# A four-layer network on one Trainium2 core: the last layer's preparation moved into the loop over layer 2's experts

## The chip, the cores and the metric

The kernel is one program on one core of a Trainium2 chip. The metric is device microseconds of one execution, the median of three runs. All data are float32. The core's engines each run their own queue of instructions: TensorE (PE, with its weight loads as PEld), VectorE (DVE), ScalarE (ACT), GpSimd (POOL) and SyncE (SP), which here only issues DMAs.

## The reference

A tensor of 16 sequences of 256 tokens with 128 features (4096 tokens) passes four layers. Each has the form `x = x + s * silu(f)`, where `s` is an attention-like branch and `f` a feed-forward branch, both computed from the same normalised `xn`. What matters here is the end of layer 2 and the whole of layer 3:

```python
# layer 2, feed-forward: mixture of 32 experts, the 4 best of a token weighted by their gate
gate = (one_hot(idx, E) * scores[..., None]).sum(-2)
h = relu(einsum('bsd,edh->bseh', x2, keys))
moe_out = einsum('bseh,ehd,bse->bsd', h, values, gate)
x = x + s * silu(src + moe_out)
# layer 3
xn = layernorm(x)
# branch s: two Mamba directions over layernorm(xn)
u = silu(conv(xn2 @ in_w)); dt = softplus(dbc[:64] @ dt_w + dt_b)
h_t = exp(dt * A) * h_{t-1} + dt * u * B_t     # 256 channels x 16 states
y = sum_n(h_t * C_t) + u * D;  s = xn + out_f + out_b
# branch f: 16 experts of 640 places, top 2 of a token, first come first served
probs = softmax(xn @ router_w + router_b);  vals, idx = top_k(probs, 2)
pos = cumsum(one_hot(idx)) - 1;  within = pos < 640
expert_inputs[idx, pos] = xn;  f = xn + shared(xn) + sum(vals * within * expert(...))
x = x + s * silu(f)
```

## The kernel before

The kernel is one class, `Net`. Four buffers of 16 KB per partition stay for the whole run: `x`, `xn`, `xnT` (features on partitions) and `s`. Tokens lie in 32 tiles of 128 (`NT`), or 8 chunks of 512 (`NCH`). Where nothing else is said, a planner orders the instructions of each engine: it goes by their order in the program, by what its own model of times says is ready, and by the buffers of the pools. Inside `manual_schedule` the named engines keep the order in which the program writes them.

**Experts of layer 2** (`ffn2`, from L1021). After attention, `norm_T` and a loop over chunks make the gates (L1045 to L1056). Then, for each chunk and each of 32 experts: one matmul to `f2_ph` (L1060), a ReLU on ACT to `f2_h` (L1064), four matmuls to `f2_po` (L1067) and four DVE sums into `acc`, weighted by the gate (L1072). `f2_ph` and `f2_po` have two buffers each, `f2_h` three. At the end of a chunk, `gate` (L111 to L113) applies SiLU and updates `x`. The planner orders all of this.

**Layer 3's first steps.** `norm_all` normalises `x` to `xn` and transposes it to `xnT` for all 32 tiles (L86 to L105). `route3` fills the DRAM buffers `xd` and `yd` with zeros and `md` with defaults (L1636, L1639, L1650), computes logits (L1669), softmax, the two best (L1682 to L1689), counts tokens per expert by two matmuls over all tiles at once (L1697, L1699) and one scan (L1707), and makes `at`, the destination row of each token and choice, and `meta`. `put_rows` (L1753) is one indirect DMA of 128 rows, issued by POOL: 64 carry rows of `xn` to `xd`, 64 rows of `meta` to `md`.

**Mamba** (`mamba3`, from L1308). It loads the weights of both directions (L69, L76), normalises `xn` a second time into `s` (L92), forms exp(A) (L1326), `taps` (L1331) and diagonals of D (L1336), issues 40 scatters, and enters a hand-written order for PE, DVE, ACT and POOL. `arrive` transposes a pair of sequences, `first` prepares one direction of a pair: it yields after each step so that a caller can place the steps. For the first direction both are run through in one go. Then the loop goes over 16 directions x 16 units; a unit has two scans (L1488, DVE), their factors two or three ahead (L1477, ACT), one product (L1462, POOL, two states ahead), one multiplication by C (L1599, DVE) and two sums on PE (L1603). Two steps of the next direction's `first` are put into each unit (`ahead`), what is left of them is put out at state 12, and one scatter goes behind every second unit. L1518 (`m_yg`) closes a direction.

**Last experts** (`ffn3`, from L1767) read `xd` and `md` and write the output.

Of the kernel before, what the change touches and what calls it, by code (L numbers as in the profile page):

```python
# [1 line left out]

# [5 lines left out]
F32 = mybir.dt.float32  # L8
# [24 lines left out]
class Net:  # L33
# [3 lines left out]
    def run(self):  # L37
        nc, tc = self.nc, self.tc
        with ExitStack() as ctx:
# [15 lines left out]
            with ExitStack() as two:  # L55
                c = two.enter_context(tc.tile_pool(name="l2c", bufs=1))
                with tc.tile_pool(name="l2a", bufs=1) as one:
                    self.norm_all()
                    bias, wqkv = self.layer1(one)
                    self.attn2(one, bias, wqkv)  # L60
                self.layer2(c)
            self.norm_all()
            self.layer3()
# [685 lines left out]
    def layer2(self, c):  # L749
        names = ("wqk2", "wv2", "wpbd", "hmask", "trig", "pe", "wo2", "ln1g", "ln1b", "ln2g", "ln2b", "selw")  # L750
        w = {n: self.load(c, n) for n in names}
        with self.tc.tile_pool(name="l2f", bufs=1) as one:
            self.ffn2(one, w)
# [267 lines left out]
    def ffn2(self, c, w):  # L1021
# [9 lines left out]
        self.relattn2(w, acc)  # L1031
        for g in range(0, NT, 8):
            self.norm(acc[:, g : g + 8, :], self.xn[:, g : g + 8, :], 8)
        with ExitStack() as ctx:
            sb = ctx.enter_context(tc.tile_pool(name="l2m", bufs=3))
            ps = ctx.enter_context(tc.tile_pool(name="l2m_ps", bufs=2, space=PSUM))
# [3 lines left out]
            for t in range(NCH):  # L1040
# [15 lines left out]
                nc.vector.tensor_tensor(gt[:, :, 0:NE], gt[:, :, 0:NE], rep[:, :, 0:NE], ALU.subtract)  # L1056
            for t in range(NCH):
                for e in range(NE):
                    ph = ps.tile([P, 512], F32, name="f2_ph")
# [3 lines left out]
                    hT = sb.tile([P, 512], F32, name="f2_h")  # L1063
# [11 lines left out]
                self.gate(sb, acc[:, 4 * t : 4 * t + 4, :], 4 * t, 4)  # L1075

# [222 lines left out]
    def layer3(self):  # L1299
        with ExitStack() as ctx:  # L1300
            keep = ctx.enter_context(self.tc.tile_pool(name="l3k", bufs=1))
            dram = ctx.enter_context(self.tc.tile_pool(name="l3x", bufs=1, space=DRAM))
            xd, md, yd, at, meta = self.route3(keep, dram)
            sent = [], []
            self.mamba3(self.scatter3(xd, md, at, meta, sent))
            self.ffn3(xd, md, yd, sent)

    def mamba3(self, scatter):  # L1308

        nc, tc = self.nc, self.tc
        N, T = 16, 2 * S
        with ExitStack() as ctx:
            c = ctx.enter_context(tc.tile_pool(name="l3c", bufs=1))
            lng, lnb = self.load(c, "lng3"), self.load(c, "lnb3")
            names = ("inT", "cb", "xpT", "dtT", "dtb", "A", "D", "outT")
            w = [{n: self.load(c, d + n) for n in names} for d in "fb"]
            one = self.ones[:, 0:1]  # L1320
            for g in range(0, NT, 8):
                self.norm(self.xn[:, g : g + 8, :], self.s[:, g : g + 8, :], 8)
            with tc.tile_pool(name="l3w0", bufs=1) as w0:
                for i, d in enumerate("fb"):
                    v = w[i]
                    nc.scalar.activation(v["A"], v["A"], AF.Exp)  # L1326
                    nc.vector.tensor_scalar_mul(v["A"], v["A"], -1.0)
                    taps = self.load_bc(w0, d + "cwr")
                    v["taps"] = c.tile([P, 4, 256], F32, name=d + "taps")
                    for j in range(4):  # L1330
                        nc.gpsimd.tensor_tensor(  # L1331
                            v["taps"][:, j, :], v["inT"][:, 0:256], taps[:, j * 256 : (j + 1) * 256], ALU.mult
                        )
                    v["Dd"] = c.tile([P, 2, P], F32, name=d + "Dd")
                    for k in range(2):
                        nc.vector.tensor_scalar_mul(v["Dd"][:, k, :], self.ident, v["D"][:, k : k + 1])  # L1336
            xp = [c.tile([P, 2, S + 3], F32, name=f"m_x{i}") for i in range(2)]
            for t in xp:
                nc.vector.memset(t[:, :, 0:3], 0.0)
            sb = ctx.enter_context(tc.tile_pool(name="l3a", bufs=2))  # L1340
            tmp = ctx.enter_context(tc.tile_pool(name="l3t", bufs=1))
            big = ctx.enter_context(tc.tile_pool(name="l3h", bufs=7))
            dram = ctx.enter_context(tc.tile_pool(name="l3d", bufs=3, space=DRAM))
            pp = ctx.enter_context(tc.tile_pool(name="l3pp", bufs=1, space=PSUM))
            factors = [pp.tile([P, 2, S], F32, name=f"m_a{n}") for n in range(3)]
            for t in factors:
                nc.vector.memset(t, 0.0)
            turn = [0]

            def arrive(p):  # L1350

                pt = pp.tile([P, 2, S], F32, name="m_pp")
                for t in range(4):
                    nc.tensor.transpose(
                        pt[:, t // 2, (t % 2) * P : (t % 2 + 1) * P], self.s[:, 4 * p + t, :], self.ident
                    )
                yield
                yield
                nc.vector.tensor_scalar(xp[0][:, :, 3:], pt, lng, lnb, ALU.mult, ALU.add)
                nc.vector.tensor_scalar(xp[1][:, :, 3:][:, :, ::-1], pt, lng, lnb, ALU.mult, ALU.add)  # L1360
                yield

            def first(p, i, st):

                v = w[i]
                uz = sb.tile([P, 4, T], F32, name="m_uz")
                u, z = uz[:, 0:2, :], uz[:, 2:4, :]
                st["u"], st["z"] = u, z  # L1370

                def inner(k):
                    pt = pp.tile([P, 2, S], F32, name="m_pp")
                    if k < 2:
                        for j in range(4):
                            nc.tensor.matmul(  # L1376
                                pt,
                                lhsT=v["taps"][:, j, k * P : (k + 1) * P],
                                rhs=xp[i][:, :, j : j + S],
                                start=j == 0,  # L1380
                                stop=j == 3,
                            )
                    else:
                        nc.tensor.matmul(
                            pt, lhsT=v["inT"][:, k * P : (k + 1) * P], rhs=xp[i][:, :, 3:], start=True, stop=True
                        )
                    return pt.rearrange("p b t -> p (b t)")
# [80 lines left out]
            def factor():  # L1468

                at = next(coming, None)  # L1470
                if at is None:
                    return
# [473 lines left out]
```

## Time and profile before

| | us |
|---|---|
| median of 3 runs | 4153.59 (4142.04 to 4166.65) |
| profiled execution, time | 4154.18 |
| profiled execution, span | 4152.5 |
| PE busy | 3635.0 (88%) |
| DVE busy | 2975.1 (72%) |
| ACT busy | 2133.2 (51%) |
| POOL busy | 1902.6 (46%) |
| layer 2's experts, L1060 to L1072 | 2325.0 to 2811.0 |
| first scan L1488 | 2940.7 |
| last multiplication by C, L1599, starts | 3928.5 |

The profile gives every instruction's engine, line, tiles, start and length, and what an idle engine waited for (`<-`). "x16" at the end of a line means that so many records were merged; a float32 matmul leaves two records, a transposition one. PEclk is the granted clock of TensorE as a share of full speed.

### The profile page before, as it was taken

How to read it: one execution, taken by the hardware profiler on the slowest of the kernel's cores; microseconds unless marked ns; L12 is line 12 of the kernel's file. 1: busy time of each engine (PE TensorE's matmuls, PEld its weight loads, DVE VectorE, ACT ScalarE, POOL GpSimd, SP SyncE). 2: the span in 40 equal slices, each digit the busy share in tenths (PEclk: the TensorE clock that was granted, in tenths of full speed). 3: DMA queues.
4: the chain of work that ended last, by engine and by line, in shares of the span. 5: the costliest groups of instructions: out<-in, count | busy, mean ns of one | idle time of the engine just before them, and what ended most of it. 6: DMA issues, size and time to landing. Idle time of an engine off the chain costs nothing.

```text
span 4152.5 us, 61388 instructions
## 1 busy us (share of the span) xinstructions
PE 3635.0 (88%) x21615; PEld 2306.3 (56%) x21615; DVE 2975.1 (72%) x6324; ACT 2133.2 (51%) x4635; POOL 1902.6 (46%) x1896
## 2 busy tenths in 40 slices
PE   5689999875999999999999999993798898899895
PEld 4477777543566666777777666662233333333353
DVE  5477777475888887666666666665698998999844
ACT  3356666642777775444445333331565665665422
POOL 5974444000444443433333000003889889877534
PEclk8899999986999999999999999995899999999998
DMA  8365554410000001000000000003211211211133
GB/s 305 126 218 180 195 198 161 59 62 6 1 1 1 1 1 41 1 1 1 1 1 1 1 1 1 1 1 132 94 70 63 82 62 62 82 62 61 56 92 102
DMA packets 87367, 268.91 MB, mean 65 GB/s; under 512 B 18176, under 2 KB 34088, under 8 KB 81555
## 3 DMA queue, kind: packets, MB, share of 16 engines
q1 hardware_dynamic: 80403, 255.46, 18.1%
q0 software_dynamic: 6656, 9.52, 0.7%
q8 instruction: 172, 2.82, 0.3%
q14 instruction: 136, 1.11, 0.1%
HBM read 192.96 MB, written 71.97 MB: 64 GB/s over the span
## 4 chain that ended last, share of the span: by engine, by line
PE 50%; DVE 25%; ACT 11%; issue 7%; POOL 5%; DMA 1%; SPq 0%; DVEq 0%; ACTq 0%; POOLq 0%
PE f_po L1067 6%; PE f_ph L1060 5%; DVE m_h L1488 4%; PE m_y L1603 4%; PE a_pp L906 3%; DVE r_mx L1164 3%; PE m_pp L1376 3%; ACT r_e L1170 2%; PE a_s L851 2%; DVE m_h L1599 2%; PE a_pp L345 2%; DVE a_e L397 2%; POOL xn_sb L170 2%; ACT m_a L1477 2%; PE r_pp L1194 2%
## 5 line engine op out<-in xcount | busy, mean ns | idle before, releaser
L1488 DVE TENSOR_TENSOR_SCAN m_h<-m_a,m_h 128x512 f32<-128x512 f32 x512 | 600.8, 1207 | 51.3 <-ACT m_a L1477 31.0
L1462 POOL TENSOR_TENSOR m_h<-m_B,m_dtu 128x1024 f32<-128x1024 f32 x256 | 597.4, 2358 | 63.6 <-PE m_y L1603 57.6
L1603 PE MATMUL m_y<-m_h,ident 128*128 128x512 f32 x1024 | 513.6, 630 | 27.0 <-DVE m_h L1599 27.0
L881 POOL TENSOR_TENSOR a_e<-a_e,a_sm 128x512 f32<-128x512 f32 x256 | 263.4, 1039 | 448.8 <-DVE a_sm L880 354.7
L1072 DVE SCALAR_TENSOR_TENSOR f_acc<-f_po,f_gate,f_acc 128x128 f32<-128x128 f32 x1024 | 277.2, 343 | 158.9 <-PE f_po L1067 158.9
L1603 PEld LDWEIGHTS m_y<-m_h,ident 128*128 128x128 f32 x1024 | 183.6, 194 | 342.6 <-issue 244.9
L397 DVE TENSOR_TENSOR a_e<-a_s,a_c 128x384 f32<-128x384 f32 x256 | 216.5, 846 | 190.5 <-PE a_s L394 188.3
L1139 POOL TENSOR_TENSOR r_g<-r_t 128x256 f32<-128x256 f32 x256 | 183.4, 728 | 360.2 <-DVE r_t L1138 358.5
L1170 ACT ACTIVATE r_e<-r_s,r_mx 128x256 f32<-128x256 f32 x512 | 207.5, 473 | 260.5 <-DVE r_mx L1164 260.4
L1599 DVE TENSOR_TENSOR m_h<-m_h,m_C 128x1024 f32<-128x1024 f32 x256 | 306.6, 1198 | 31.1 <-PE m_C L1498 31.1
L1138 DVE TENSOR_TENSOR r_t<-r_pp,trig_sb 128x512 f32<-128x512 f32 x256 | 169.2, 682 | 207.0 <-PE r_pp L1129 205.8
L1064 ACT ACTIVATE f_h<-f_ph 128x512 f32<-128x512 f32 x256 | 152.8, 597 | 299.9 <-PE f_ph L1060 290.8
L1067 PEld LDWEIGHTS f_po<-values_sb,f_h 128*128 128x128 f32 x2048 | 240.6, 193 | 97.2 <-ACT f_h L1064 89.5
L874 ACT ACTIVATE a_e<-a_e,a_mx 128x256 f32<-128x256 f32 x512 | 255.1, 500 | 54.5 <-DVE a_sm L880 48.2
L1067 PE MATMUL f_po<-values_sb,f_h 128*128 128x128 f32 x2048 | 264.9, 283 | 5.8 <-DVE f_acc L1072 4.9
L402 ACT ACTIVATE a_e<-a_e,a_mx 128x128 f32<-128x128 f32 (+1 forms) x512 | 218.6, 454 | 89.7 <-DVE a_mx L398 66.0
L1158 PE MATMUL r_s<-pe_sb,r_g 128*128 128x256 f32 x1024 | 260.7, 388 | 0.0
L372 POOL COPY a_st<-a_p 128x192 f32<-128x192 f32 x256 | 135.1, 530 | 243.3 <-PE a_s L393 160.6
L1060 PE MATMUL f_ph<-xnT_sb,keys_sb 128*128 128x512 f32 x512 | 241.7, 594 | 0.0
L1477 ACT ACTIVATE m_a<-m_dt,bA_sb 128x510 f32<-128x510 f32 x256 | 170.9, 686 | 132.9 <-DVE m_h L1488 132.1
L1498 PE MATMUL m_C<-m_dbc,ident 32*128 32x512 f32 x512 | 148.9, 654 | 86.1 <-DVE m_h L1599 86.1
L1477 ACT ACTIVATE m_a<-m_dt,fA_sb 128x510 f32<-128x510 f32 x256 | 169.9, 685 | 105.8 <-DVE m_h L1488 104.5
(459 smaller groups left out, 8239.8 us busy)
## 6 DMA issues: line engine op xcount, KB each, us to landing
m_B<-m_rows SPq DMA_DIRECT2D x32, 2048.0 KB
a_p<-pc SPq DMA_DIRECT2D x32, 768.0 KB
a_c<-cs SPq DMA_DIRECT2D x32, 768.0 KB
cs<-a_es SPq DMA_DIRECT2D x64, 256.0 KB
pc<-a_es SPq DMA_DIRECT2D x64, 256.0 KB
a_p<-pc SPq DMA_DIRECT2D x32, 512.0 KB
a_c<-cs SPq DMA_DIRECT2D x32, 512.0 KB
cs<-bg SPq DMA_DIRECT2D x8, 768.0 KB
```

The costliest lines, as they stand in the source:

```text
L397: nc.vector.tensor_tensor(e, s[h], c2s[m // 2][:, :, x], ALU.add)
L881: nc.gpsimd.tensor_tensor(e, e, bc(sm, S), ALU.mult)
L1060: nc.tensor.matmul(ph, lhsT=keys[:, e, :], rhs=self.xnT[:, t * 512 : (t + 1) * 512], start=True, stop=True)
L1067: nc.tensor.matmul(po[:, k, :], lhsT=hT[:, k * P : (k + 1) * P], rhs=values[:, e, :], start=True, stop=True)
L1072: nc.vector.scalar_tensor_tensor(acc[:, n, :], po[:, k, :], gate[:, n, e : e + 1], acc[:, n, :], ALU.mult, ALU.add)
L1158: nc.tensor.matmul(s[h][:, i, :], lhsT=G[:, i * P : (i + 1) * P], rhs=w["pe"], start=False, stop=i == 1)
L1170: nc.scalar.activation(e[:, i, :], s[h][:, i, :], AF.Exp, bias=mx[:, i : i + 1])
L1462: nc.gpsimd.tensor_tensor(h, st["B"][n // 8][:, m : m + 2, :], bc1(st["dtu"][:, k, :], 2), ALU.mult)
L1477: nc.scalar.activation(f[:, :, 1:], sts[d]["dt"][:, k, :].rearrange("p (b t) -> p b t", b=2)[:, :, 1:], AF.Exp, scale=w[work[d][1]]["A"][: ...
L1488: nc.vector.tensor_tensor_scan(h[:, j, :], ready.pop(0), h[:, j, :], 0.0, op0=ALU.mult, op1=ALU.add)
L1599: nc.vector.tensor_tensor(h, h, sts[d]["C"], ALU.mult)
L1603: nc.tensor.matmul(sts[d]["y"][k], lhsT=self.ident, rhs=h[:, j, :], start=False, stop=n + j == N - 1)
```

## The change

`norm_all`, `route3`, `scatter3` and the preparing part of `mamba3` are taken away as stages. Two objects take their place. `Route3` makes the buffers, fills them, and has `tiles(k0, n)`: norm, second norm, transposition, routing and destinations of `n` tiles, in steps with a yield after each. The second norm is no longer computed from `xn`'s statistics: its factor follows from the variance of `x` (`rs[:, 1]`), and POOL multiplies. Counts per expert are kept from block to block in `before`. `Mamba3` makes the weights and has `arrive` and `first` as before. Both are set up behind the gates of layer 2 and ahead of its experts. During the experts, one step is taken per expert: tiles 0 to 15 in chunk 4, the first Mamba direction in chunk 5, tiles 16 to 27 in chunk 7; from expert 8 of a chunk on, one scatter per expert, if one is waiting. Tiles 28 to 31 are routed in the Mamba loop, ahead of the second direction's steps. In PSUM, the three factors and one bank (`m_pp`) are taken for the experts' stage too, in the place of the banks of the gates. `layer2`'s pool `l2c` moves to the right side and is released after attention. `l3a` (two buffers) becomes one pool per direction, the two halves of B likewise.

```diff
     def ffn2(self, c, w, left, last):
...
         self.relattn2(w, acc)
+        left.release()
...
-        with ExitStack() as ctx:
-            sb = ctx.enter_context(tc.tile_pool(name="l2m", bufs=3))
-            ps = ctx.enter_context(tc.tile_pool(name="l2m_ps", bufs=2, space=PSUM))
+        with tc.tile_pool(name="l2n", bufs=3) as sb, tc.tile_pool(name="l2n_ps", bufs=2, space=PSUM) as ps:
...
+        route = Route3(self, last)
+        mamba = Mamba3(self, last)
+        with ExitStack() as ctx:
+            sb = ctx.enter_context(tc.tile_pool(name="l2m", bufs=2))
+            ps = ctx.enter_context(tc.tile_pool(name="l2m_ps", bufs=2, space=PSUM))
+            along = {4: route.tiles(0, 16, mamba), 5: mamba.begin(), 7: route.tiles(16, 12, mamba)}
             for t in range(NCH):
                 for e in range(NE):
+                    next(along.get(t, iter(())), None)
+                    if e >= 8:
+                        route.scatter()
                     ph = ps.tile([P, 512], F32, name="f2_ph")
...
-                    hT = sb.tile([P, 512], F32, name="f2_h")
+                    hT = sb.tile([P, 512], F32, name="f2_h", bufs=3)
...
                 self.gate(sb, acc[:, 4 * t : 4 * t + 4, :], 4 * t, 4)
+                for _ in along.pop(t, ()):
+                    pass
+        return route, mamba
...
+    def tiles(self, k0, n, mamba):
...
+        for k in range(n):
+            nc.vector.bn_stats(st[:, k, :], net.x[:, k0 + k, :])
+            nc.vector.bn_aggr(mv[:, k, :], st[:, k, :])
+            if k % 4 == 3 and k + 1 < n:
+                yield
...
+        nc.scalar.activation(rs, rs, AF.Sqrt)
+        nc.vector.reciprocal(rs, rs)
+        for k in range(n):
+            nc.vector.tensor_scalar(
+                net.xn[:, k0 + k, :], net.x[:, k0 + k, :], mv[:, k, 0:1], rs[:, 0, k : k + 1], ALU.subtract, ALU.mult
+            )
+            if k % 4 == 3:
+                yield
+        for k in range(0, n, 4):
+            k4 = slice(k0 + k, k0 + k + 4)
+            nc.gpsimd.tensor_tensor(net.s[:, k4, :], net.xn[:, k4, :], bc(rs[:, 1, k : k + 4], D), ALU.mult)
+        for k in range(0, n, 4):
+            t = mamba.bank()
+            for j in range(4):
+                nc.tensor.transpose(t[:, j * P : (j + 1) * P], net.xn[:, k0 + k + j, :], net.ident)
+            yield
+            nc.scalar.copy(net.xnT[:, (k0 + k) * P : (k0 + k + 4) * P], t)
+            yield
...
+            nc.tensor.matmul(pl[:, k, :], lhsT=net.xnT[:, o : o + P], rhs=self.rw, start=True, stop=True)
...
+        nc.scalar.activation(l, l, AF.Exp)
+        nc.vector.tensor_reduce(mx, l, AX.X, ALU.add)
...
+        for q, m in ((pin, self.tri), (tot, net.ones)):
+            nc.tensor.matmul(q, lhsT=m, rhs=mask, start=True, stop=True)
+        yield
...
+        nc.vector.tensor_copy(run[:, 0, :], self.before)
+        for k in range(n):
+            nc.vector.tensor_tensor(run[:, k + 1, :], run[:, k, :], tot[:, k, :], ALU.add)
+        nc.vector.tensor_copy(self.before, run[:, n, :])
...
+        self.todo += [(i, k, j) for k in range(k0, k0 + n) for j in range(2) for i in range(2)]
+        yield
+
+    def scatter(self):
+        if self.todo:
+            i, k, j = self.todo.pop(0)
+            rows = self.meta[:, j, k, :] if i else self.net.xn[:, k, :]
+            self.net.put_rows((self.xd, self.md)[i], self.at[:, j, k : k + 1], rows, self.sent[i])
...
+    def begin(self):
+        yield from self.arrive(0)
+        yield from self.first(0, 0, self.sts[0])
...
-            for _ in range(40):
-                next(scatter)
...
-            for f in (arrive(0), first(*work[0], sts[0])):
-                for _ in f:
-                    pass
...
                     ahead = first(*work[d + 1], sts[d + 1]) if d + 1 < len(work) else behind(d)
+                    if d == 0:
+                        ahead = chain(route.tiles(28, 4, self), ahead)
...
                 if k:
-                    next(scatter, None)
+                    route.scatter()
```

## The prediction

> **What bounds the kernel now.** I read the table of stages first, then the order of time inside the expert stage and at both ends of the stretch behind it, then the waits and the per-direction marks of the Mamba loop. The stages, 50 us each (columns: stretch, length, then busy us and instructions of PE, PEld, DVE, ACT, POOL, then PE clock, DMA share, GB/s):
>
> ```profile
> 2700.00:2750.00 50.00, 50.00 (x271) 33.23 (x269) 32.74 (x124) 17.54 (x29) 0.00 (x0) 1.00 0.00 1
> 2800.00:2850.00 50.00, 33.53 (x150) 26.60 (x148) 37.12 (x265) 14.51 (x29) 3.55 (x6) 0.66 0.47 192
> 2850.00:2900.00 50.00, 2.42 (x6) 1.53 (x7) 19.79 (x48) 1.95 (x4) 27.33 (x30) 0.52 0.27 80
> 2900.00:2950.00 50.00, 26.88 (x37) 8.51 (x37) 10.03 (x10) 22.32 (x27) 38.01 (x29) 0.64 0.27 103
> 2950.00:3000.00 50.00, 45.65 (x114) 17.29 (x113) 43.54 (x40) 32.62 (x43) 41.11 (x22) 0.99 0.23 91
> ```
>
> The experts (2325 to 2811) hold PE at 50.00 of 50; DVE, ACT and above all POOL have room. The Mamba loop (from 2941) is paced by DVE. Between them no engine is full: it is a chain of single steps. Its two ends, in order of time:
>
> ```profile
> 2809.89 1.13 DVE L1072 SCALAR_TENSOR_TENSOR f_acc<-f_po,f_gate,f_acc 128x128 f32<-128x128 f32 x4 [1.50 <-PE f_po L1067]
> ...
> 2864.55 0.18 DVE L1748 CAST f_at<-f_ab 128x64 int32<-128x64 f32 x1
> ...
> 2897.87 2.79 POOL L1331 TENSOR_TENSOR ftaps<-finT_sb,fcwr_bc 128x256 f32<-128x256 f32 x4
> ...
> 2940.66 4.64 DVE L1488 TENSOR_TENSOR_SCAN m_h<-m_a,m_h 128x512 f32<-128x512 f32 x4 [13.87 <-POOL m_h L1462]
> ```
>
> From the last expert sum (end 2811.0) to the first scan (2940.7) 129.6 us pass: 53.5 of norms and routing, 33 in which POOL issues scatters before it reaches the taps, 43 of the first direction's preparation. And one pair of experts inside the stage:
>
> ```profile
> 2797.06 0.60 ACT L1064 ACTIVATE f_h<-f_ph 128x512 f32<-128x512 f32 x1 [2.21 <-PE f_ph L1060]
> 2797.71 2.05 PE L1067 MATMUL f_po<-values_sb,f_h 128*128 128x128 f32 x16
> 2797.92 0.60 ACT L1064 ACTIVATE f_h<-f_ph 128x512 f32<-128x512 f32 x1 [0.26 <-PE f_ph L1060]
> 2798.90 2.16 DVE L1072 SCALAR_TENSOR_TENSOR f_acc<-f_po,f_gate,f_acc 128x128 f32<-128x128 f32 x8 [1.50 <-PE f_po L1067]
> 2799.49 0.30 PEld L1060 LDWEIGHTS f_ph<-xnT_sb,keys_sb 128*128 128x128 f32 x2
> 2799.60 1.88 PE L1060 MATMUL f_ph<-xnT_sb,keys_sb 128*128 128x512 f32 x4
> 2800.72 0.60 ACT L1064 ACTIVATE f_h<-f_ph 128x512 f32<-128x512 f32 x1 [2.21 <-PE f_ph L1060]
> ```
>
> Two experts take 3.66 us (2797.06 to 2800.72), PE without a gap. ACT is idle 2.21 us once per pair, DVE 1.5. The ReLU ends 0.1 to 0.2 us before PE needs it, so ACT has a window and no slack outside it.
>
> **What goes.** The 129.6 us. What must still happen behind the last expert: the gate's SiLU (0.63), one table load (1.28) and a factor (0.69) on ACT, beside it on POOL the first product (2.36, L1462), whose buffer comes free with the last experts. The scan then starts some 3.2 us after the last sum. Gain 126.4. The cover for the moved SP and POOL work is the idle of both in the expert stage: nine zero-fill DMAs (in the stretch they ran from 2815 to 2837 at 409 to 423 GB/s; the expert stage moves 1 GB/s), 21 weight loads at 0.43 each on SP, memsets, iotas, eight tap multiplications of 0.7 and 76 scatters at 1.27 apart on POOL. At nothing; without that cover they cost what POOL paid above, 33 us and more.
>
> **What PE gets.** The stage is PE's, so all of it adds, at the prices of the full clock: 28 transposes at 0.13 (L1018, eight in 1.04) 3.6; 28 routing matmuls at 0.245 (f_pg L1045, four tiles in 0.98; the routing row L1669 ran at half clock) 6.9; the counts, 256 and 192 columns against 0.94 for 512, 1.7; Mamba: 4 transposes 0.5, and 14 matmuls of 512 columns at 0.94, 13.2. Sum 26.
>
> **What DVE gets there.** 16 tiles: statistics 0.26 and norm 0.26 a tile, max and replace 0.25 a tile, some 35 operations on 16x16 per row at about 0.33 (half of the 0.60 apart of 512 wide): 23 us in chunk 4; 12 tiles 18 us in chunk 7. A chunk's 128 sums and gate are 36 us of about 66 with PE's additions, so it fits. The work is cut into steps, one per expert; a step of about 1 us twice a pair exceeds the 1.5 by half a us, which the two f_po buffers take. At nothing; and the first norm of 24 tiles (12.5 us) was in this stage already.
>
> **What ACT gets there.** Eight copies of 0.58, two square roots, two softmax exponentials, and Mamba's 15 us with four table loads; in all nine loads and about five to return to SiLU. Row: the load at 2963.38 takes 1.28 and the SiLU behind it starts at 2964.68, so a switch costs 1.3. The Trainium skill ("ScalarE: Activation LUTs", What ACT_TABLE_LOAD costs) puts a switch at some 1.28 for the load and 1.38 for a drain, 2.66 in all. By the page no switch fits into the window of 2.21, and fourteen of them would hold PE for about 0.9 each, 12 us more; by the row they fit. I take the row. What doesn't fit even so: exponential and logarithm with two loads (4.8 us, over by 2.6), two SiLU of 2.34 (over by 0.1 each), and about 24 short operations, of which half meet a ReLU and delay it by some 0.4. Sum 8; bounds 0 (all land in windows) and 25 (each holds PE for its own length once).
>
> **What the Mamba loop gets.** Tiles 28 to 31 are routed inside its first direction. DVE there is the pace: norms 2.1, softmax and top two 1.9, some 30 small operations at 0.12, together 7.8. The order is by hand here, and two steps have DVE read at once what ACT has just been given (square root with two table loads, exponential): 4 us of waiting, during which the scans queued behind wait, and PE's sums and ACT's factors behind those. Then the second direction's preparation: it has 22 steps, and 23 slots before unit 12 forces the rest out. The routing takes 11 of these; 10 steps come in one burst. In it DVE's m_r waits for matmul, ReLU, Abs and a loaded exponential (about 3.2 us net), and the next factors queue on ACT behind logarithm, copies, SiLU and two loads (about 4.5): 8 once. POOL's four steps end about 14 us on, before the 16 us at which DVE wants the next products; the spread for that direction leaves around unit 10 and needs about 8. No trace shows this burst; bounds 0 and 20, value 8 from the steps of the lone chain (2920 to 2936).
>
> Against that the scatters. Before, 88 of 128 fall into the loop, one per two units, up to about 3620. The close of every second direction:
>
> ```profile
> 3381.86 0.68 DVE L1518 TENSOR_TENSOR m_yg<-m_y,m_uz 128x512 f32<-128x512 f32 x1
> ...
> 3508.17 0.68 DVE L1518 TENSOR_TENSOR m_yg<-m_y,m_uz 128x512 f32<-128x512 f32 x1
> ...
> 3634.47 0.68 DVE L1518 TENSOR_TENSOR m_yg<-m_y,m_uz 128x512 f32<-128x512 f32 x1
> ...
> 3756.41 0.68 DVE L1518 TENSOR_TENSOR m_yg<-m_y,m_uz 128x512 f32<-128x512 f32 x1
> ```
>
> 126.3 with 16 scatters, 121.9 without: 0.28 each. Now chunk 4 gives out 7, chunks 5 and 6 24 each, chunk 7 9 and 12: 76; the loop keeps 52. 36 fewer save 10 (bounds 3 and 12: the first pair, with scatters of the wide rows, took only 123.4).
>
> **The sum.** 4152.5 - 129.6 + 3.2 + 26 + 8 + 7.8 + 4 + 8 - 10 = 4069.9, and 1.7 around the span (this execution took 4154.18): 4072. The median of the runs shown, 4153.59, is the same as this execution within 0.6, so the forecast needs no shift. With the bounds: down to about 4042, up to 4115.
>
> **Rivals.** (A) *A wait on the weights enters the expert stage.* Exp on A (ACT) and the D diagonals (DVE) stand ahead of the experts in the program, and now their loads are issued right behind 9.2 MB of zeros, not 40 us later. If the planner places them before the data lands, ReLU or sums queue behind them for up to the 22 us of the fill and some 6 of loads; the same with a transposition placed too early on PE. For it: in the stretch ACT waited 17.9 us at that very line. Against: the planner put the taps behind 26 scatters, to 2897.9, where the weights' DMA traffic had ended by 2880, so it reckons loads long. Time 4085 to 4130, say 4103.
> (B) *Slower: the pairs of experts break up.* If added steps make PE's order ph, po, ph, po, each expert shows PE the wait for its ReLU: 0.75 us, as the last, unpaired one does at 2808. In the 72 experts with steps that is 54; over all 256 it is 192, giving about 4256. It decides from about 110 unpaired experts. Against: the two f_ph and f_po buffers and three f_h stay, and chunks 0 to 3, 6 have no steps.
> (C) *The work isn't hidden.* If the planner lets the second block's routing slip behind the last expert, its chain of about 18 us shows again: 4090. Against: its 21 steps end by expert 21 of 32.
>
> **How the numbers follow.** Sum as reckoned 0.58 (4042 to 4100); A 0.16; C 0.10; B in part, ending within 0.5% of 4154, 0.05; B in full or a cost in the loop that I don't see, slower, 0.11. What a measurement of this kernel can tell from no change is about 0.5%, 21 us. Faster by more than that 0.84, within 0.05, slower 0.11. The range 4040 to 4130 holds the sum, A and C, and leaves the last two.
>
> **What would show it.** Right: experts from about 2325 to 2845, first scan within 5 us of the last sum, POOL busy with scatters in chunks 5 to 7, one direction of about 85 us (65 before) and then pairs of 126 until about the sixth direction, 122 after. Wrong: ACT or DVE waiting for a DMA in the first chunk (A), PE idle before every f_po (B), routing lines after the last f_acc (C). A stage of experts over 550 us, or a loop longer than before by over 40, would refute the sum.

## The result, and the profile after

The changed kernel took 4174.5 us (median of 9 runs, 4169.2 to 4186.3), the kernel before 4151.9 (9 runs): a ratio of 1.0056, 95% interval 1.0040 to 1.0072. The prediction was 4072, faster. The gap behind the experts went, as forecast; more than its worth came back in other stages, two of which (the first two rows below) the sum held at no change.

Time by stage, from marks in the traces. The profiled execution of the changed kernel was 10 us above its median, so a second profile of it, with a span of 4174.3, stands in the table. "Three edits" is the version that the experiments led to.

| stage (marks) | before | changed | three edits | predicted difference |
|---|---|---|---|---|
| start to the norm ahead of layer 2's attention (`f2_acc` from `xn`) | 1645.1 | 1673.4 (+28.3) | 1641.2 (-3.9) | 0 |
| to the first expert sum | 699.4 | 707.6 (+8.2) | 699.1 (-0.3) | 0 |
| first to last expert sum | 466.2 | 544.0 (+77.8) | 510.4 (+44.2) | +34 |
| last expert sum to first scan | 130.0 | 5.7 (-124.3) | 5.1 (-124.9) | -126.4 |
| first scan to first `m_yg` | 65.1 | 104.2 (+39.1) | 104.9 (+39.8) | +19.8 |
| first to last `m_yg` | 926.6 | 917.8 (-8.8) | 922.1 (-4.5) | -10 |
| rest | 220.1 | 221.6 (+1.5) | 220.1 (0.0) | 0 |
| sum | 4152.5 | 4174.3 (+21.8) | 4102.9 (-49.6) | -82.6 |

The stretches that were shown of before, in the profile of the changed kernel (same columns: length, busy us and instructions of PE, PEld, DVE, ACT, POOL, then PE clock, DMA share, GB/s):

```profile
2700.00:2750.00 50.00, 37.95 (x180) 23.40 (x179) 16.94 (x62) 19.30 (x27) 38.11 (x40) 0.93 0.23 70
2750.00:2800.00 50.00, 15.22 (x72) 10.82 (x73) 10.03 (x41) 9.20 (x14) 27.52 (x25) 0.63 0.04 12
2800.00:2850.00 50.00, 50.00 (x272) 33.31 (x271) 32.52 (x122) 16.76 (x28) 0.00 (x0) 1.00 0.00 1
2850.00:2900.00 50.00, 49.14 (x284) 34.76 (x284) 35.58 (x130) 20.34 (x34) 3.30 (x4) 1.00 0.01 1
2900.00:2950.00 50.00, 38.61 (x196) 25.52 (x196) 40.61 (x168) 16.11 (x24) 23.88 (x18) 0.91 0.16 51
2950.00:3000.00 50.00, 27.37 (x61) 11.20 (x60) 42.79 (x81) 12.23 (x19) 23.77 (x16) 0.71 0.01 3
```

A chunk of experts with its extra work still holds PE at 50.00 or 49.14. The hole is at 2737 to 2783, beside a POOL that does nothing but 40 scatters in 50 us. The other weak stretch is the loop's first direction, where DVE is at 42.79 of 50 and PE at 27.37. The ends of what was the gap, in order of time:

```profile
2933.04 2.16 DVE L1083 SCALAR_TENSOR_TENSOR f_acc<-f_po,f_gate,f_acc 128x128 f32<-128x128 f32 x8 [0.28 <-PE f_po L1078]
2935.24 0.63 ACT L112 ACTIVATE gate_t<-f_acc 128x512 f32<-128x512 f32 x1 [2.68 <-DVE f_acc L1083]
2940.55 2.34 DVE L1799 TENSOR_TENSOR_SCAN m_h<-m_a,m_h 128x512 f32<-128x512 f32 x2 [3.24 <-POOL m_h L1773]
```

From the end of the last sum to the first scan 5.4 us, for 129.6. The hole inside the experts, from the waits of that profile (us in total, times, longest) and in order of time:

```profile
PE f_po L1078 <- ACT f_h L1075: 52.9, 3, 44.9
ACT m_a L1788 <- POOL m_dt L1734: 44.3, 1, 44.3
DVE m_r L1561 <- POOL m_e L1728: 41.7, 1, 41.7
```

```profile
2691.65 1.19 POOL L1322 DMA_INDIRECT f_xd<-xn_sb,f_at  x1 [48.20 <-DVE f_acc L1083]
...
2734.89 1.28 ACT L1788 ACT_TABLE_LOAD   x1
...
2772.12 0.95 POOL L1322 DMA_INDIRECT f_md<-f_meta,f_at  x1 [0.31 <-issue]
2773.09 2.35 POOL L1728 TENSOR_TENSOR m_e<-m_e,m_r 128x1024 f32<-128x1024 f32 x1
2775.48 0.17 DVE L1561 COPY m_r<-f_before 128x16 f32<-128x16 f32 x1 [41.71 <-POOL m_e L1728]
...
2780.49 1.91 ACT L1788 ACTIVATE m_a<-m_dt,fA_sb 128x510 f32<-128x510 f32 x3 [44.32 <-POOL m_dt L1734]
...
2782.97 3.78 PE L1078 MATMUL f_po<-values_sb,f_h 128*128 128x128 f32 x16 [44.95 <-ACT f_h L1075]
```

`scatter()` stands once per expert in the program. The planner took the 64 scatters of the first 16 tiles as soon as their destinations were there and issued them in one row, 1.26 us apart, from 2691.65 to 2773.1. The first direction's e - r (L1728) stands behind the row. With it dt is late; and the planner had put the loop's first decay factors (L1788) into ACT's queue ahead of ReLUs, and DVE's next routing copy, which needs the same buffer, ahead of sums. Both engines of the experts wait for POOL.

The period of the loop, as before:

```profile
3419.37 0.68 DVE L1829 TENSOR_TENSOR m_yg<-m_y,m_uz 128x512 f32<-128x512 f32 x1
...
3541.33 0.68 DVE L1829 TENSOR_TENSOR m_yg<-m_y,m_uz 128x512 f32<-128x512 f32 x1
...
3663.29 0.69 DVE L1829 TENSOR_TENSOR m_yg<-m_y,m_uz 128x512 f32<-128x512 f32 x1
```

A pair takes 122.0 from 3419 on. Before, it took 126.3 until 3634.

### The profile page after: what moved, and what is told of

Same layout as the page of the kernel before. It is cut to its first block, busy times and chain, and to the rows that moved or that the text cites. A ratio compares the mean times of both kernels' runs of the same rounds, so it can differ in the third digit from the quotient of the medians.

```text
span 4182.7 us, 61271 instructions
## 1 busy us (share of the span) xinstructions
PE 3630.1 (87%) x21623; PEld 2307.2 (55%) x21623; DVE 2976.5 (71%) x6273; ACT 2129.8 (51%) x4623; POOL 1910.6 (46%) x1911
## 4 chain that ended last, share of the span: by engine, by line
PE 49%; DVE 25%; ACT 11%; issue 7%; POOL 6%; DMA 2%; SPq 0%; ACTq 0%; DVEq 0%; POOLq 0%
PE f_po L1078 5%; PE f_ph L1071 4%; PE m_y L1911 4%; DVE m_h L1799 4%; DVE r_mx L1178 3%; PE a_pp L908 3%; PE m_pp L1676 2%; ACT r_e L1184 2%; DVE m_h L1907 2%; PE a_s L853 2%; PE a_pp L346 2%; DVE a_e L398 2%; POOL xn_sb L171 2%; PE r_s L1161 2%; ACT m_a L1788 2%
## 5 line engine op out<-in xcount | busy, mean ns | idle before, releaser
L1788 ACT ACTIVATE m_a<-m_dt,fA_sb 128x510 f32<-128x510 f32 x256 | 170.0, 686 | 165.1 <-DVE m_h L1799 119.5
L1788 ACT ACTIVATE m_a<-m_dt,bA_sb 128x510 f32<-128x510 f32 x256 | 170.9, 686 | 132.1 <-DVE m_h L1799 131.2
```

Of the source, the lines that this page charges most:

```text
L1788: nc.scalar.activation(f[:, :, 1:], sts[d]["dt"][:, k, :].rearrange("p (b t) -> p b t", b=2)[:, :, 1:], AF.Exp, scale=w[work[d][1]]["A"][: ...
```

## Experiments

Each is the kernel named, with the edit shown (`no_sync` and `sync` stand for the long names of the two kinds of dependency: an order in one queue alone, or a wait). Times are medians; ratios are taken against runs of the kernel before beside it (4147 to 4152).

**The move of one pool, alone, on the kernel before.**

```diff
-                c = two.enter_context(tc.tile_pool(name="l2c", bufs=1))
+                c = two.enter_context(tc.tile_pool(name="l2c", bufs=1, side="right"))
```

> The kernel before with one word of the change: the pool l2c (layer 2's weights and sums) allocated on the right side. Nothing of the last layer is moved. Theory (the pool's move alone lets the planner put the 4 MB write of line and its rpe load ahead of the first layer's small load of upb on SP's queue): upb's load is issued behind line's and lands some 35 us later, attention of layer 2 starts about 44 us later (1078 for 1034), and the median is about 4152 + 44 = 4196 (4185 to 4205). Rival (the 44 us of the changed kernel come from its later parts, or are an accident of that profile): attention starts at 1034, and the time stays within 10 us of 4152.

Measured: 4178.6, ratio 1.0077 (1.0055 to 1.0099): 29.5 us slower than the runs beside it (4149.1). The first waits of this profile around 750 us are those of the changed kernel:

```profile
DVE bf_bs L213 <- DMA upb_sb<-in_upb: 31.7, 1, 31.7
PE bf_pb L216 <- DVE bf_bs L213: 33.3, 1, 33.3
```

On SP's queue the 4 MB write of `line` and the `rpe` load that it needs now stand ahead of the 2 KB load of `upb`; before, they stood behind layer 1's weights. First the kernel before, then this one:

```profile
747.03 0.25 SPq L69 DMA_DIRECT2D upb_sb<-in_upb  x1
...
764.83 0.65 SPq L772 DMA_DIRECT2D line<-a_line  x1
```

```profile
741.86 0.67 SPq L772 DMA_DIRECT2D line<-a_line  x1
747.36 6.92 SPq L69 DMA_DIRECT2D upb_sb<-in_upb  x1
```

The feed-forward of layer 0 waits for that load. That `line`'s buffers come free earlier once the pool no longer lies on the left is my reading of why the planner does this; it wasn't tried separately. The size was 30, not the 44 of my expectation: that was read off a profile of the changed kernel whose middle ran slower than its median runs.

**The same, undone in the changed kernel.** `line`'s write is held behind the loads of `upb`, `bcon` and `dnb` in SP's order:

```diff
             d = nc.sync.dma_start(line, bc1(ln, P))
+            for q in self.first_loads:
+                tc.add_manual_dep(d.ins, q.ins.name, no_sync, reason="line behind")
```

> The changed kernel with the write of line held behind the loads of upb, bcon and dnb in SP's order; all else as it is. Theory: the 44 us before attention of layer 2 go, its first projection starts at 1034 to 1040, and the median is 4174 - 40 = 4134 (4128 to 4145). Rival (line must be written anyway and its 4 MB only wait elsewhere, since the bias is gathered from it): the start moves by under 10 us and the median stays over 4160.

Measured: 4181.7. The norm mark moved from 1673.4 to 1643.3, two us under before, as the theory has it, and the time did not move: the expert stage was 584 us for 544. This looked like the rival and was not; see the chips below.

**Scatters paced.** Each scatter of the expert stage waits for the last sum of the expert before it:

```diff
                     if e >= 8:
-                        route.scatter()
+                        route.scatter(added)
...
-                        nc.vector.scalar_tensor_tensor(
+                        added = nc.vector.scalar_tensor_tensor(
...
     def scatter(self, behind=None):
...
+                self.net.tc.add_manual_dep(self.sent[i][-1].ins, behind.ins.name, sync, reason="paced")
```

> The changed kernel with every scatter of the expert stage waiting for the accumulate of the expert before it, so that the planner can't issue 64 of them in a row; the rest of the order is the planner's. Theory (the row of scatters on POOL holds e - r of the first direction, with it dt, with it the decay factor that ACT has in its order ahead of ReLUs: 45 us of idle TensorE): no wait over 10 us is left in the expert stage, its length falls from 547 to about 502, and the median is 4174 - 45 = 4130 (4120 to 4140). Rival (the scatters only show a wait that the table switches, DVE's extra work and the weights would cause anyway): the stage stays over 535 and the median over 4162.

> The changed kernel with each scatter of the expert stage behind the accumulate of the expert before it, on the same chip as the run before. Paced scatters have cost the same on every chip so far: 4140 (4135 to 4146) in either case.

Measured: 4140.5, ratio 0.9985 (0.9976 to 0.9993), and in the second run, on another chip, 4144.1 (0.9987). The stage is 512.7 us, no wait of PE there exceeds 6.7. Against the changed kernel's 4174.5 that is 34 us less; 45 were expected. The two ran on chips that treat a row differently (below), so the 34 alone is not the row's price.

**The experts' pools ahead of the gates'.** `l2m` and its PSUM are opened before `l2n`, so that the first experts don't wait for the gates' banks.

> The changed kernel with the pools of the expert stage (l2m and its PSUM) opened ahead of the gates' pools, so that the first experts need not wait for the gates' banks; the Mamba factors' banks then wait for those. Theory (the 16 us by which the experts start later than the rest of the shift explains come from the PSUM pools being opened in turn): the first expert's ReLU starts 16 us earlier (2372 for 2388), the median is 4174 - 16 = 4158 (4150 to 4165). Rival (the 16 us come from the zero fills and loads of the last layer, 225 GB/s there): start and median unchanged within 5 us.

Measured: 4211.1; the first ReLU did start earlier (2356.9; the changed kernel's second profile 2378.2, at the same norm mark within 1.1), and the stage took 582.8 us. Again the start moved and the end did not.

**Edits together.** First order and pacing, then the pools too:

> The changed kernel with both edits that were tried alone: line behind the three small loads, and each scatter of the expert stage behind the accumulate of the expert before it. Theory (the 30 us of the pool's move and the row of scatters are two separate costs; alone, the first gain was lost because the row of scatters held the experts for the whole of its 81 us): 4140.5 - 29.5 = 4111 (4103 to 4120), TensorE's signals come within 9 us of each other all through the stage. Rival (the end of the expert stage is set by something that does not move with its start): 4135 to 4142 again.

> As the run with both edits, and the expert stage's pools opened ahead of the gates' pools. Theory (the first experts start 18 us earlier, as in the run with that edit alone, and without the row of scatters nothing takes it back): 4111 - 18 = 4093 (4086 to 4102). Rival (what starts earlier waits for the weights or for the last layer's set-up instead): within 5 us of the run with both edits.

Measured: 4114.0 (0.9912, 0.9893 to 0.9930) and 4101.7 (0.9885, 0.9864 to 0.9906). With the scatters paced, the 30 us of the pool's move come back almost whole (4140.5 to 4114.0). The pools' order gave 12 by the medians, and the runs of the two don't overlap (4109.2 to 4120.9, 4100.7 to 4104.6); but by the marks it is 5 (2.1 at the start, 3.3 in the stage), and the rest lies in layers that the edit doesn't touch. Its worth stays open between these.

**Routing of tiles 28 to 31 moved.** In the version with three edits, into the last quarter of the loop's second direction, where no step stood:

```diff
-                            ahead = behind(d)
+                            ahead = route.tiles(28, 4, self) if d == 1 else behind(d)
...
-                    if d == 0:
-                        ahead = chain(route.tiles(28, 4, self), ahead)
```

> As the run with three edits, and the routing of tiles 28 to 31 taken out of the first direction of the loop and put into the last quarter of the second, where nothing else stands. Theory (of the 39 us that the first direction grew, 11 are its DVE work, 10 are four small DVE operations that wait for a GpSimd product, and 18 are waits of steps that are drained at once): the 18 go, the rest moves with the work: first direction near 66, the second longer by 15 to 20, 4093 - 15 = 4078 (4070 to 4088). Rival (the second direction pays the same): within 6 us of the run with three edits.

Measured: 4095.0, ratio 0.9870 (0.9848 to 0.9892), the fastest version by its median. That is 6.7 under the version that it was made from: outside the theory's range and at the edge of the rival's. The first direction fell from 104.9 to 65.9; the second rose from 61.0 to 82.6 and the third from 65.4 to 73.9. Of 39 us, 30 moved with the work and 9 were due to the place, not 18.

**The factors behind the ReLUs.** In the changed kernel, the first three decay factors are held behind the last ReLU on ACT, the row stays.

> The changed kernel with the first three decay factors (L1788, ACT) held behind the last ReLU of the experts in ACT's order; the row of scatters stays. Theory (the scatters on POOL are the cause: with ACT free, DVE's copy at L1561 still waits for the same e - r, and the accumulates behind it): the time stays within 10 us of 4174. Rival (the hoisted factor alone holds the ReLUs): 45 us less, near 4130, and no wait over 10 us in the expert stage.

> The changed kernel with the first three decay factors behind the last ReLU in ACT's order, once more, since the first run of it fell on a chip where the long row holds the experts by itself. On a chip where the row's landing records are whole: if the hoisted factor alone holds the ReLUs, near 4130 to 4140; if DVE's copy at L1561, which waits for the same step on POOL, holds the accumulates as well, 4164 to 4176. On a chip where they are thin: near 4220 again, and the question stays open.

Measured: 4219.8 and 4213.3; the first is slower than either theory, the second what was expected of a chip of the kind described next. On such chips the edit changes nothing in the stage (584.7 and 583.8; the changed kernel there 584.0). What the hoisted factors cost by themselves stays open.

**The row of scatters by itself.** In the version with three edits, all 64 scatters go out at once in chunk 6, where POOL has nothing else to do and nobody waits for POOL:

```diff
                     if t == 7 and e >= 8:
                         route.scatter(added)
+                    for _ in range(64 if (t, e) == (6, 8) else 0):
+                        route.scatter(added)
```

> The run with three edits (4101.7), but with the 64 scatters of the first 16 tiles issued in one row in chunk 6, behind an accumulate of that chunk, where POOL has nothing else to do and no expert waits for POOL. Theory (a row costs only what stands behind it on POOL): within 8 us of 4102, TensorE busy all through the row. Rival (a row of scatters 1.26 us apart also delays the signals of the other engines, as the records of three runs hint, where TensorE's signals came up to 39 us apart beside the row): experts lose 40 us or more beside the row, 4140 or more, with waits on TensorE's results of over 10 us.

Measured: 4179.0, 77 us more than the version it was made from. My theory, that a row costs only what stands behind it on POOL, fell on this chip. The stretch beside the row, first of this kernel, then of the paced version (its profile on another chip):

```profile
2750.00:2800.00 50.00, 7.57 (x20) 4.67 (x20) 3.38 (x12) 1.19 (x2) 37.86 (x40) 0.58 0.09 27
```

```profile
2750.00:2800.00 50.00, 49.14 (x281) 34.13 (x280) 35.62 (x131) 18.69 (x31) 20.62 (x23) 1.00 0.05 13
```

And what the engines of the row's kernel wait for there:

```profile
2776.86 2.07 PE L1088 MATMUL f_po<-values_sb,f_h 128*128 128x128 f32 x8 [2.83 <-ACT f_h L1085]
2778.72 3.62 PE L1081 MATMUL f_ph<-xnT_sb,keys_sb 128*128 128x512 f32 x4
2798.53 1.12 DVE L1093 SCALAR_TENSOR_TENSOR f_acc<-f_po,f_gate,f_acc 128x128 f32<-128x128 f32 x4 [32.47 <-remote]
...
2823.79 1.09 ACT L1085 ACTIVATE f_h<-f_ph 128x512 f32<-128x512 f32 x2 [46.99 <-remote]
```

PE ended f_ph at 2782.3; the ReLU that needs only this started at 2823.8. In the trace's semaphore events (a semaphore is the counter by which one engine signals another), PE's increments beside the row stand still for 19, 27 and 22 us one after the other; in the running stage ahead of it no gap exceeds 7.2. So the engines stood although what they waited for had ended. That the signals were late is my reading of it: the profile names no releaser (`remote`).

**Program or chip?** The changed kernel's own profile had no such late signals. It was run again unaltered. Beside it ran the three edits with the 64 scatters released in four groups of 16, one at every eighth expert of chunk 6; then both, the long row and the paced version on one further chip:

> The changed kernel, unaltered, beside the runs of this study. In the five altered programs that kept the row of 64 scatters, TensorE's signals came up to 44 us apart during the row, and the expert stage was 583 to 586 us; in the profile of the changed kernel the signals were on time until ACT began to wait, and the stage was 544 us. Theory (the difference belongs to the program, however it is laid out): 4174 again (4168 to 4186), stage 544. Rival (it belongs to the execution or the chip): near 4215, stage 584.

> The run with three edits (4101.7), but with 64 scatters in four rows of 16, each behind the accumulate of every eighth expert of chunk 6. A row of 16 at 1.26 us is 20 us long. Theory (it takes some 15 us of back-to-back scatters before signals are delayed, as in the long row, where TensorE was on time for the first 12 to 17): each row costs 0 to 6 us, 4102 to 4126. Rival (every back-to-back scatter costs the experts its own 1.26 us): 4 x 20 = 80 us, near 4180.

> The changed kernel once more, on one chip with the next three. In the two profiles of the changed kernel so far, and in that of the four rows of 16, each of the first 72 scatters left its 16 landing records (1152) and no signal of TensorE was late beside a row; in all others a part of the records is missing beside dense scatters (228 of 1152 with the long row), and there the row held the experts. Theory P (it belongs to the program): 4174, stage 544, records whole. Theory C (it belongs to the chip or the session): the four kernels of this call are alike in this: either all whole, and this one 4174; or all thin, and this one near 4215 with a stage of 584.

> The long row in chunk 6 (4179 before) on the same chip. Theory P: 4179 again, records thin, stage 586. Theory C: with whole records it costs nothing and the time is near 4102 (4096 to 4110); with thin records 4179.

> The four rows of 16 (4098 before) on the same chip. Theory P: 4098 again, records whole. Theory C: with whole records 4098; with thin records the rows, which in the trace follow each other almost without a break, hold the experts, 4140 to 4180.

> The three edits (4101.7 before) on the same chip, with the scatters one for each expert. Both theories: 4098 to 4103, since the paced scatters cost the experts nothing in either case.

Measured (landing records: semaphore events of the scatters' queue in the whole trace):

| kernel | median | expert stage | landing records |
|---|---|---|---|
| changed, its first runs | 4174.5 | 544.3 | 3344 |
| changed, again | 4174.0 | 544.0 | 3344 |
| four groups of 16, same chip | 4098.4 | 507.6 | 3344 |
| changed, further chip | 4233.0 | 584.0 | 1703 |
| long row, that chip | 4173.5 | 583.1 | 1741 |
| four groups of 16, that chip | 4155.8 | 561.1 | 1854 |
| three edits, that chip | 4101.7 | 510.2 | 2390 |

The groups did not stay apart on the first of these chips. Sixteen scatters take 20 us and eight experts some 15, so all 64 went out in one row, 2727.2 to 2807.2, 1.26 us apart. It held nobody:

```profile
2750.00:2800.00 50.00, 49.88 (x288) 35.15 (x287) 34.19 (x131) 19.37 (x33) 37.92 (x40) 1.00 0.10 27
```

This is the row of the long-row kernel, 40 scatters in these 50 us, with PE at 49.88 in place of 7.57. On this chip my theory stands, and what the changed kernel's row costs here is what waits behind it on POOL: the stage is 544.0 with it and 507.6 with a row in chunk 6, 36 us, of which the pools' order has some 3. On the further chip the groups held the experts, and so came 8 to 11 us apart.

It does not belong to the program: the same one takes 4174 on one chip and 4233 on another (ratio there 1.0178, 1.0147 to 1.0209). Of the 59 us, by the two profiles, 40 are in the stage and 14 ahead of layer 2's attention, where no row is. Landing records tell the two kinds apart. Where they are missing ("thin"), a row holds the experts for about as long as it lasts: 584.0 against 512.7, and the long row costs 77 and 72 over the paced version's 4101.7. The other runs with a row (`line` behind, pools first, factors behind) were all on chips with thin records, 1685 to 1715, and had stages of 583 to 585. Read against a changed kernel that takes 4233 on one such chip and, by its 4174.5 and the 40 us of stage, an estimated 4215, the 4181.7 above is a gain after all and the 4211.1 may be one; by how much isn't measured, since the changed kernel did not run on that chip.

Three things stay open. Every paced version ran on chips with thin records (2344 to 2390 of 3344; the profile of before has 2315), so a paced one was not measured where they are whole. Apart from one chip with thin records, which was used three times, each chip was used once, so what differs may be the chip or what else went on at that time. And whether the recording of the profile takes part, since its records go missing where engines stand, was not tried.

**Small DVE operations beside GpSimd.** In the changed kernel, 64 operations of 128x16 of no use, in six forms, one per unit in the loop's fifth to eighth direction:

> The changed kernel with 64 small DVE operations of no use, one behind each multiplication by C in the loop's fifth to eighth direction, in six forms of 128x16 in turn: copy and sum of two from SBUF alone, copy and sum with PSUM as a source, maximum-like reduction and reciprocal from SBUF. Theory (copies and sums with SBUF sources alone wait for a GpSimd product that is running): those two forms take 0.15 to 0.2 us where POOL is idle and end with the product where it runs, up to 2.3 us for one product and more for two in a row; the four others take 0.15 to 0.25 us everywhere. Rival (every small DVE operation beside a product is slowed, or the four slow ones had another cause): all six forms alike.

Measured, in the order of the form lines (duration in ns: least, median, most):

```profile
L1912 DVE COPY f_before<-ones x11: 159/1170/5221, 3292.8 to 3547.3; 128x16 f32<-128x16 f32 x11
L1914 DVE TENSOR_TENSOR f_before<-ones x10: 160/732/1864, 3302.1 to 3529.7; 128x16 f32<-128x16 f32 x10
L1916 DVE COPY f_before<-m_C x11: 159/160/168, 3277.9 to 3537.0; 128x16 f32<-128x16 f32 x11
L1918 DVE TENSOR_TENSOR f_before<-m_C,ones x11: 158/163/167, 3289.4 to 3543.9; 128x16 f32<-128x16 f32 x11
L1920 DVE TENSOR_REDUCE f_before<-ones x10: 153/156/163, 3297.5 to 3533.5; 128x1 f32<-128x16 f32 x10
L1922 DVE RECIPROCAL f_before<-ones x11: 236/238/245, 3283.9 to 3540.4; 128x16 f32<-128x16 f32 x11
```

Copy and sum from SBUF alone take 0.16 us or up to 5.2; with PSUM as a source, the same operations never leave 0.16. The theory holds: every copy or sum of the first two forms that took over 0.2 started beside a product and ended 0.03 to 0.04 us after it. (4254 in one run on a chip with thin records; its time carries the row as well.)

## Why the prediction was wrong, point by point

The profile of the changed kernel is 104 us over the sum. By stage, 28 of it are the move of the pool, 8 the stretch with the gates, 34 the row of scatters, 10 the experts' other work, 19 the first direction, and 5 the rest; the 34 is the stage of 544.0 less the 510.4 of three edits. The 8 are in part noise (701.3 in the first profile for 707.6) and went with the pools' other order (698.4).

**What went: right.** Gain 126.4 forecast, 124.3 measured.

**Layers 0 and 1: missing.** The sum has no term for the pool's move to the right side; I had read it as bookkeeping. It cost 29.5 us, two layers ahead of anything that I looked at.

**"At nothing" for 76 scatters on POOL: wrong, and the largest failed step.** I took their times from the program (one per expert, chunk by chunk) and their cover from POOL's idle time. The planner issued 64 in a row, and POOL's idle time was no cover for what stands behind them. The price, by the stage: 36 us where records are whole (544.0 against 507.6, with the row in chunk 6), some 71 where they are thin (584.0 against the paced version's 512.7 and 513.7). On the first kind the failed step is the cover; on the second a row costs that much even with nothing behind it, and why stays open. The sign was in the trace of before, in a line that I quoted: the planner had put 26 scatters ahead of the taps, and I used it only as evidence on the weights' DMA.

**PE 26 and ACT 8 in the experts: 34 forecast, 44 measured** with the three edits. In that profile PE waits 20.7 us in the stage, against 5.8 before: 15 for the 8. In the second profile of the same version it waits 14.3, at a stage of 510.2, so how the 10 us too much divide between PE and ACT is not firm. The largest that both have is one wait of 6.75 that I had not seen at all, because it comes from the loop: the decay factor that the planner put among the ReLUs waits for dt even in this version.

```profile
2677.85 1.28 ACT L1735 ACT_TABLE_LOAD   x1
2679.14 1.15 ACT L1735 ACTIVATE m_l<-m_e,ones 128x1024 f32<-128x1024 f32 x1
...
2681.96 1.28 ACT L1800 ACT_TABLE_LOAD   x1
2689.97 1.30 ACT L1800 ACTIVATE m_a<-m_dt,fA_sb 128x510 f32<-128x510 f32 x2 [6.73 <-POOL m_dt L1746]
```

The same lines settle the rule that was weighed: the function starts 1.29 us after its load began, so the row (1.3) was right and the 2.66 of the Trainium skill ("ScalarE: Activation LUTs", What ACT_TABLE_LOAD costs) is not seen here.

**The first direction: 19.8 forecast, 39.1 measured.** It rose by three terms. DVE's own operations were 12.5 by their durations, for 7.8. The waits in it were 22.6 us for 6.4 before, 16 more for the 12 forecast:

```profile
DVE m_r L1727 <- ACT m_e L1722: 7.4, 1, 7.4
DVE m_h L1799 <- ACT m_a L1788: 5.9, 2, 4.9
DVE m_h L1907 <- PE m_C L1809: 3.7, 1, 3.7
```

The first is the burst of the second direction's steps, where it was expected and near its 8. The third term, 10 us, was missing. Four small operations, not among the 12.5, took 10.8 us together, where their kind takes 0.15 to 0.22. Two of them, beside POOL's products:

```profile
2967.07 4.64 POOL L1773 TENSOR_TENSOR m_h<-m_B,m_dtu 128x1024 f32<-128x1024 f32 x2
2968.30 0.23 DVE L1528 TENSOR_TENSOR m_e<-m_pp,rb_bc 128x64 f32<-128x64 f32 x1 [2.92 <-PE m_pp L1523]
2968.82 2.99 DVE L1530 TENSOR_TENSOR m_e<-m_e,m_r 128x64 f32<-128x64 f32 x1
...
2979.37 2.34 POOL L1773 TENSOR_TENSOR m_h<-m_B,m_dtu 128x1024 f32<-128x1024 f32 x1 [6.48 <-PE m_y L1911]
2979.80 1.95 DVE L1561 COPY m_r<-f_before 128x16 f32<-128x16 f32 x1
```

L1530 ends at 2971.81 and the products at 2971.71; L1561 at 2981.75 and its product at 2981.71; the other two (L1497, 4.11 us, and L1564, 1.71) end 0.04 after a product as well. L1528, of the same size but from PSUM, passes through in 0.23. The Trainium skill ("SBUF — State Buffer", SBUF: two separate sides) says it beforehand: DVE and GpSimd share a pair of ports, one of them holds it for a whole instruction, and on DVE's side it concerns operations with two SBUF inputs and those in a two-port mode. This case agrees, with the numbers above. In the stage of the gap POOL had been idle beside these operations, so the trace of before showed nothing; in the loop POOL multiplies for 4.7 of each 7.6 us, and that could have been asked.

**Scatters in the loop: right.** 10 us fewer forecast, 8.8 measured, with the period of 122.0.

**Its other figures.** The sum comes out as written. The bounds that it states add to 4054 and 4108, not 4042 and 4115, and B in full, 192 on 4072, is 4264, not 4256; none of this changes the outcome.

**The rivals.** A (weights), B (pairs broken up) and C (work behind the last expert) did not come: in the first chunk neither ACT nor DVE waits for a DMA, plain chunks hold PE at 50.00, and the last sum is followed by the gate. The slower end that came had none of these mechanisms. All three rivals looked for lateness of the moved work itself; none for what the moved work would delay on the queue that it was moved to. "A stage of experts over 550 us would refute the sum": on the one kind of chip it was 544, on the other 584.

## What to carry to other kernels

Where a planner orders queues, "once per expert" in the program is a wish: read the issue times, and if work must be spread, tie each piece to something that advances with the stage; the three edits with paced scatters took 4101.7 on both chips that they ran on, where the long row took 72 to 77 more. Such a tie holds only if the stage is slower than the pieces: groups of 16 behind every eighth expert ran together into one row. Idle time of an engine covers moved work only if nothing that others need stands behind it in that engine's queue. Moving a pool changed the order of the DMA queue two layers ahead, for 29.5 us: compare that order in all stages, not only where the change is. And before a difference between two kernels is explained, run both on the same chip: here one program differed by 59 us between two.

## What the runs showed of the hardware that was not expected

- Beside 64 indirect DMAs 1.26 us apart, with nothing behind them on POOL, engines of two chips stood for over 40 us after the matmul that they needed had ended, and the kernel took 4179.0 and 4173.5 for 4101.7; on another chip the same row held nobody (PE 49.88 of 50, 4098.4). One scatter per expert, 1.3 and 2.4 us apart in turn, left no wait of PE over 6.8 us on the chips where a row did; on the other kind it was not run.
- A copy of 128x16 on DVE took 0.16 to 5.2 us, depending on whether GpSimd was multiplying; a copy from PSUM 0.16 to 0.17 always.
